# A recommender's attention over 200 history rows on Trainium2: another share of rows by address, categories by products, longer loop bodies and a new end

## The chip, the cores and the metric

The kernel runs on one core of a Trainium2 chip. The metric is device microseconds (us) of one execution, lower is better. The kernel before has a median of 31,307.11 us over 12 runs (31,251.07 to 31,361.09).

Engines have these short names: PE (matrix products; PEld is its loading of weights), DVE (VectorE), ACT (ScalarE), POOL (GpSimd), SP (SyncE, which here only issues DMAs). SBUF is the memory on the chip that the engines work from, and PSUM the memory that PE writes to. A DMA is issued by an engine and then runs by itself.

## The reference

The model has a user, an item, a category and 200 earlier items for each of B = 16,384 examples. The tables have rows of D = 64 fp32 numbers (256 bytes): 100,000 items, 100,000 users, 1,000 categories. All is fp32.

```python
def dice(x, alpha, axis):
    mean = jnp.mean(x, axis=axis, keepdims=True)
    var = jnp.var(x, axis=axis, keepdims=True)
    p = jax.nn.sigmoid((x - mean) * jax.lax.rsqrt(var + EPS))
    return x * (p + alpha * (1.0 - p))
u = u_emb[user]                # (B, 64)
it = i_emb[item]               # (B, 64)
c = c_emb[cate]                # (B, 64)
h = i_emb[hist]                # (200, B, 64)
itb = jnp.broadcast_to(it[None], h.shape)
feat = jnp.concatenate([h, itb, h - itb, h * itb], axis=-1)
a = dice(feat @ au_W1 + au_b1, au_alpha, axis=1)     # 256 -> 36
w = a @ au_W2 + au_b2                                # 36 -> 1
cur = jnp.sum(w * h, axis=0)
z = jnp.concatenate([u, it, c, cur], axis=-1)        # (B, 256)
z = dice(z @ W1 + b1, alpha1, axis=0)                # 256 -> 80
z = dice(z @ W2 + b2, alpha2, axis=0)                # 80 -> 40
return z @ W3 + b3                                   # 40 -> 2
```

The mean and variance of the first `dice` go over the whole batch, for each of the 200 history positions by itself. So no gate of a position can be computed before all 16,384 rows of that position have been through the first layer.

## The kernel before, in words

**Tiles and steps.** A position is called l here, 0 to 199. Its 16,384 rows are eight columns c = 0 to 7 of 16 tiles, 128 rows a tile. A step is k = l x 8 + c, 1,600 in all. The rows of a step land in `rows[k % 5]` (`ROWS` = 5), a buffer of 128 partitions x 16 tiles x 64 numbers.

**Two ways to fetch.** (1) *Gathers*: `gather` (L123) is one indirect DMA on POOL's queue, which fetches 128 rows by a list of row numbers in SBUF. (2) *By address*: in `rows_by_address` (L279) an engine loads row addresses into its registers (`values_load_multi_w_load_instructions`, L293, up to `LOAD` = 20 addresses a load) and issues one DMA of 256 bytes for each row (L301). Half of these rows are issued by SP, half by ACT. They land in `side[m % 3]`, 128 rows a tile m, and each adds 16 to the semaphore `landed[m % 3]`. `SIDES` = (1, 3, 4, 5, 6, 7) are the columns whose sixteenth tile goes by address; the tile of column `SOMETIMES` = 5 does so in one of three l only (`has_side`, L315; `EACH` = 3), and otherwise it is gathered by a list of its own, `sidx`. So an l has 6 tiles by address and 122 gathers, or 5 and 123. The 768 or 640 rows by address of an l are split evenly over its eight steps, 96 or 80 a step, half of them SP's and half ACT's: 48 in three loads of 16 addresses, or 40 in two of 20 (a load that would cross from one tile to a tile that doesn't follow it in memory is split).

`await_rows` (L309) waits on ACT until a tile has landed and clears its semaphore; `place` (L346) then copies the tile from `side` to its place in `rows` on ACT (L352).

**One step** (`step`, L383) issues, in this order, for three steps and one far behind: the gathers of k; the bias of step k - 2 (`hidden`, ACT L339, from PSUM `px` to `xs`), and behind the last column of an l its `measure` and `moments`; the sigmoid of step k - 9 (`gate`, ACT L328, `LAG` = 9); the landed tile of k - 1 (`place`); the rows by address of k; for k - 1 the transposes (`turn`, DVE L156) and the first products (L161, PSUM `ph` and `px`); the statistics of k - 2 (`measure`, DVE L344); for k - 1 the product of h and item and its matmul (`product`, L359 to 361); the weights of k - 9 and their sum into `curT` (`weights`, `weigh`, L331, L335, L336). Each engine works through its own part of this list in order. So the ACT queue has, for each step: one `hidden`, one `gate`, possibly one wait with a copy, and its row issues.

`moments` (L363) makes mean and variance of one l from the statistics of its 16 halves on DVE and calls `scale_and_shift` (L167), which takes the square root on ACT (L170) and the reciprocal on DVE.

**The loop.** A hardware loop (`For_i`, L457) runs bodies of `LPB` = 45 l, written out in full: four bodies make 180 l. The last 20 l are written out behind the loop. All engines meet at the end of each body.

**Before the loop** (L425 to 454): row numbers of items, categories and users are loaded (`ids`), attention weights are arranged (`attention_weights`), 128 gathers fetch the item rows, DVE transposes them into `itT`, and the weights of the head are loaded (`head_weights`, DMAs on SP).

**After the loop** (from L486): the last 20 l, then 256 gathers for categories and users (`head_fetch`, L471, one step of 16 tiles for each column and table), the layer 256 -> 80 (`head_layer`, L477), its two `dice` (`head_moments` L503, once for 64 and once for 16 of the 80 units; `dice` L522), the layer 80 -> 40, its `dice`, the last layer, transposes back, and the output in 14 DMAs at the very end (L562, L568).

Of the kernel before, what the change touches and what calls it, by code (L numbers as in the profile page):

```python
# [14 lines left out]
P = 128  # L15
D = 64
# [4 lines left out]
LPB = 45  # L21
# [7 lines left out]
LOAD = 20  # L29
# [5 lines left out]
def din_kernel(  # L35
# [76 lines left out]
    ids = [make(f"ids{i}", P, NT, dt=I32) for i in range(3)]  # L112
# [17 lines left out]
    def load_ids(t, v):  # L130
        nc.sync.dma_start(t[:, :NC], columns(v))
        for s in range(NS):
            nc.sync.dma_start(t[:, NC + s : NC + s + 1], col(v[(NC + s) * P : (NC + s + 1) * P]))

# [9 lines left out]
    def load_addresses(i, l):  # L144
        nc.sync.dma_start(addr[i], r_hist[ds(l, 1), NC * P :])
# [21 lines left out]
    def scale_and_shift(mean, var, rstd, shift):  # L167
        n = mean.shape[0]
        std = small.tile([P, 1], F32, tag="std", name="std")
        nc.scalar.activation(std[:n], var, AF.Sqrt, bias=eps[:n])  # L170
        nc.vector.reciprocal(rstd, std[:n])
        nc.vector.scalar_tensor_tensor(shift, mean, -1.0, rstd, ALU.mult, ALU.mult)

    eps = make("eps", P, 1)
# [14 lines left out]
    def attention_weights():  # L189
        nc.vector.memset(eps, EPS)  # L190
# [45 lines left out]
    def head_weights():  # L236
# [3 lines left out]
        for e in range(2):  # L240
            for g in range(2):
                r, d = quarter(e, g), ts(e, S)
                nc.sync.dma_start(w1a[r, :, ts(g, ZA)], w1[d, :, :ZA])
                nc.sync.dma_start(w1b[r, :, ts(g, ZB)], w1[d, :, ZA:])
        for g in range(2):
            nc.sync.dma_start(w2a[ts(g, ZA), g * ZA : g * ZA + Z2], W2[:ZA])
# [20 lines left out]
    flat = i_emb.rearrange("v d -> (v d)").bitcast(U8)  # L267

# [4 lines left out]
    def tiles_by_address(l):  # L273

        round_, i = divmod(l, EACH)
        first = round_ * (EACH * (NS - 1) + 1) + i * (NS - 1) + (i > 0)
        return first, [j for j, c in enumerate(SIDES) if has_side(l * ND + c)]

    def rows_by_address(k):  # L279
        l, s = divmod(k, ND)  # L280
        first, tiles = tiles_by_address(l)
        n = len(tiles) * P // ND // 2
        loads = -(-n // LOAD)
        for i, (engine, issue) in enumerate(
            ((mybir.EngineType.SP, nc.sync), (mybir.EngineType.Activation, nc.scalar))
        ):
            r0, end = (2 * s + i) * n, (2 * s + i + 1) * n
            while r0 < end:
                many = min(end - r0, -(-n // loads))
                at0 = tiles[r0 // P] * P + r0 % P  # L290
                while tiles[(r0 + many - 1) // P] * P + (r0 + many - 1) % P != at0 + many - 1:
                    many -= 1
                _, at = nc.values_load_multi_w_load_instructions(  # L293
                    addr[l % 3][:, at0 : at0 + many],
                    engines=(engine,), min_val=0, max_val=ROW * (V - 1),
                    skip_runtime_bounds_check_because="the DMA checks the address against the table",
                )
                for r, a in enumerate(at, r0):
# [9 lines left out]

    def await_rows(m):  # L309
        if m in keys:  # L310
            fence = nc.scalar.wait_ge(landed[m % 3], 16 * P)
            tc.declare_fence(fence.ins, group=keys.pop(m))
            nc.scalar.sem_clear(landed[m % 3])

    def has_side(k):  # L315
        l, c = divmod(k, ND)
        return c in SIDES and (c != SOMETIMES or l % EACH == 0)
# [28 lines left out]
    def place(k):  # L346
        if has_side(k):
            l, c = divmod(k, ND)
            first, tiles = tiles_by_address(l)
            m = first + tiles.index(SIDES.index(c))  # L350
            await_rows(m)
            nc.scalar.copy(rows[k % ROWS][:, TD - 1], side[m % 3])  # L352
# [30 lines left out]
    def step(k, last=None):  # L383
# [12 lines left out]
        if has(k - LAG):  # L396
            gate(k - LAG)
        if has(k - 1):
            place(k - 1)
        if has(k):  # L400
            rows_by_address(k)
        if has(k - 1):
# [5 lines left out]
        if has(k - LAG):  # L408
# [3 lines left out]
    def steps(l0, n, end):  # L412
        for k in range(n * ND):
            l, c = divmod(k, ND)
            if c == 0 and l + 1 < end:
                load_hist_ids((l + 1) % IDX, l0 + l + 1)
                if (l + 1) % EACH:
                    load_side_ids((l + 1) % IDX, l0 + l + 1)
            if c == 2 and l + 1 < end:
                load_addresses((l + 1) % 3, l0 + l + 1)  # L420
            if c == 4 and l + 1 < end:
                scale_addresses((l + 1) % 3)
            step(k)

    with tc.manual_schedule():  # L425
        load_ids(ids[0], r_item)
        load_hist_ids(0, 0)
        load_addresses(0, 0)
        load_ids(ids[1], r_cate)
        load_ids(ids[2], r_user)  # L430
        nc.gpsimd.iota(lanes, pattern=[[1, P]], base=P, channel_multiplier=-1)
        attention_weights()
        for t in (*hT, *xs, *side, hm):
            nc.vector.memset(t, 0.0)  # L434
        for t in curT:
# [7 lines left out]
        scale_addresses(0)  # L443
        layer(px, [(blk_m, hm)])

        for c in range(ND + 1):
            if c < ND:
                for n in range(TD):
                    j = column(c, n)
                    gather(rows[c % ROWS], ids[0][:, j : j + 1], n, i_emb)  # L450
            if c:
                transpose(itT[c - 1], rows[(c - 1) % ROWS])
        nc.vector.memset(rows[-1 % ROWS], 0.0)
# [13 lines left out]
    def measure_head(i, j, t):  # L467
        for h in range(2):
            nc.vector.bn_stats(zst[i][:, 2 * j + h, :], t[:, ts(h, CH)])

    def head_fetch(k, j):  # L471
        c, u = divmod(j, 2)
        for n in range(TD):
            i = column(c, n)
            gather(rows[k % ROWS], ids[1 + u][:, i : i + 1], n, (c_emb, u_emb)[u])

    def head_layer(j):  # L477
        c, u = divmod(j, 2)
        if u == 0:
# [121 lines left out]
```

## Time and profile before

| what | number |
|---|---|
| median of 12 runs | 31,307.11 us |
| the profiled execution's own time | 31,272.79 us |
| its span, first to last instruction | 31,271.0 us |
| granted TensorE clock | 0.805 of full speed |
| gathers of history rows by `idx` / by `sidx` | 24,400 / 133 |
| gathers by `ids` (items, categories, users) | 3 x 128 |
| rows issued by address, SP / ACT | 68,288 / 68,288 |
| DMA engines, mean busy share | about 0.1; 28 GB/s from HBM |
| start of the last gather | 31,167.99 us |

How to read the profile: each engine has a row of busy time, its share of the span, and its number of instructions; a group of instructions is named by its line, engine, operation and output <- inputs. Idle time is put down to what ended it, "<-". "issue" is idle time in which the engine waited for nothing that the profile shows, its own preparation of the next instruction among it. `ACTq` and `SPq` are the DMA queues that ACT and SP feed; a row of such a queue in the timeline gives the start, the length and the number of issues of one uninterrupted stretch. The times of PE's and POOL's instructions are partly modelled; starts are more exact than lengths.

The four joins between bodies show on POOL as longer distances between two gathers: 27.52, 5.29, 5.71 and 4.10 us.

### The profile page before, as it was taken

What the parts mean: (1) busy time and instruction counts of PE and PEld (TensorE: products, weight loads), DVE (VectorE), ACT (ScalarE), POOL (GpSimd) and SP (SyncE); (2) the same over time, 40 slices, a digit from 0 to 9 for tenths busy, and PEclk for the clock granted to TensorE, in tenths of its full rate; (3) what the DMA queues carried; (4) which work ended last, traced back from release to release, by engine and by line L of the source; (5) the groups of instructions that cost most, each with busy time, mean ns of one, the idle gap of its engine ahead of it and who ended that gap; (6) DMA issues with size and microseconds to landing.
All of it is one profiled execution on the core that took longest, in us unless ns stands there. A gap on an engine that the chain in (4) does not pass through costs nothing. (4 is left out here: it accounts for less than half of the span.)

```text
span 31271.0 us, 423966 instructions
## 1 busy us (share of the span) xinstructions
PE 20699.5 (66%) x38856; PEld 8494.9 (27%) x38856; DVE 15126.9 (48%) x18955; ACT 4403.3 (14%) x4941; POOL 23526.3 (75%) x24922
## 2 busy tenths in 40 slices
PE   5666666666666666666666666666666666666666
PEld 2222222222222222222222222222222222222222
DVE  4444444444444444444444444444444444444444
ACT  1111111111111111111111111111111111111111
POOL 7777777777777777777777777777777777777776
PEclk8878877887788788887888878878878888877887
DMA  1111111111111111111111111111111111111111
GB/s 29 29 29 29 29 29 29 29 29 28 29 29 29 29 29 29 29 29 29 29 29 29 29 29 29 29 29 29 29 29 29 29 29 29 29 29 29 29 29 24
DMA packets 1130924, 894.71 MB, mean 29 GB/s; under 512 B 729024, under 2 KB 729024, under 8 KB 1127896
## 3 DMA queue, kind: packets, MB, share of 16 engines
q0 software_dynamic: 797344, 818.07, 11.8%
q1 hardware_dynamic: 193112, 31.56, 0.6%
q10 hardware_dynamic: 137440, 17.76, 0.4%
q14 instruction: 2722, 22.30, 0.2%
q8 instruction: 306, 5.01, 0.1%
HBM read 865.10 MB, written 0.13 MB: 28 GB/s over the span
## 5 line engine op out<-in xcount | busy, mean ns | idle before, releaser
L123 POOL DMA_INDIRECT rows<-in_L_rec_i_emb,idx x24400 | 23037.9, 944 | 7486.6 <-issue 7213.7
L161 PE MATMUL ph<-hT,unit 128*128 128x512 f32 x6404 | 5890.2, 1067 | 10372.5 <-DVE hT L156 10370.6
L335 DVE SCALAR_TENSOR_TENSOR wb<-wb,au_bias,hT 128x1024 f32<-128x1024 f32 x1609 | 2079.7, 1293 | 10852.8 <-PE wb L161 10852.8
L156 DVE STREAM_TRANSPOSE hT<-rows 64x512 f32<-64x512 f32 x6404 | 4515.1, 705 | 2591.5 <-ACT rows L352 1877.1
L339 ACT ACTIVATE xs<-px,au_bias 128x1024 f32<-128x1024 f32 x1602 | 1783.5, 1113 | 25585.4 <-issue 11742.9
L161 PEld LDWEIGHTS ph<-hT,unit 128*128 128x128 f32 x6404 | 1722.5, 302 | 13401.0 <-DVE hT L156 13234.8
L161 PE MATMUL px<-hT,blk_h 128*128 128x512 f32 x6404 | 4111.5, 731 | 0.1
L161 PE MATMUL px<-itT,blk_i 128*128 128x512 f32 x6404 | 3338.4, 603 | 0.0
L161 PE MATMUL wb<-y,blk_p 128*128 128x512 f32 x6436 | 3295.2, 594 | 29.8 <-DVE y L331 29.8
L161 PE MATMUL wb<-xs,blk_x 128*128 128x512 f32 x6436 | 3293.3, 593 | 5.3 <-DVE curT L336 5.3
L161 PE MATMUL px<-hm,blk_m 128*128 128x512 f32 x6408 | 3013.0, 592 | 40.6 <-DVE hm L434 40.6
L360 DVE TENSOR_TENSOR hm<-ph,itT 128x1024 f32<-128x1024 f32 x1601 | 1960.2, 1224 | 1903.3 <-PE ph L161 1903.3
L161 PEld LDWEIGHTS px<-hT,blk_h 128*128 128x128 f32 x6404 | 1644.2, 257 | 2407.3 <-issue 2398.3
L344 DVE BATCH_NORM_STATS2 st<-xs 128x6 f32<-128x512 f32 x3204 | 2060.5, 685 | 290.6 <-ACT xs L339 245.7
L336 DVE TENSOR_TENSOR curT<-wb,curT 128x1024 f32<-128x1024 f32 x1609 | 1969.7, 1224 | 54.8
L331 DVE TENSOR_TENSOR y<-pg,xs 128x1024 f32<-128x1024 f32 x1609 | 1952.8, 1214 | 2.3 <-ACT pg L328 2.2
L161 PEld LDWEIGHTS px<-itT,blk_i 128*128 128x128 f32 x6404 | 1395.8, 218 | 2024.0 <-issue 2024.0
L328 ACT ACTIVATE pg<-xs,sh,rs 128x1024 f32<-128x1024 f32 x1609 | 1934.3, 1202 | 22.4 <-DVE y L331 17.4
L161 PEld LDWEIGHTS wb<-y,blk_p 128*128 128x128 f32 x6436 | 1224.9, 190 | 1575.3 <-issue 1539.7
L161 PEld LDWEIGHTS px<-hm,blk_m 128*128 128x128 f32 x6408 | 1217.9, 190 | 1573.3 <-issue 1532.7
L161 PEld LDWEIGHTS wb<-xs,blk_x 128*128 128x128 f32 x6436 | 1223.7, 190 | 1550.5 <-issue 1541.1
L352 ACT COPY rows<-side 128x64 f32<-128x64 f32 x1068 | 249.2, 233 | 328.9 <-DMA side<-in_L_rec_i_emb 197.2
(155 smaller groups left out, 2190.5 us busy)
## 6 DMA issues: line engine op xcount, KB each, us to landing
side<-in_L_rec_i_emb SPq DMA_DIRECT2D x68288, 0.2 KB
side<-in_L_rec_i_emb ACTq DMA_DIRECT2D x68288, 0.2 KB
rows<-in_L_rec_i_emb,idx POOLq DMA_INDIRECT x24400
idx<-in_r_hist SPq DMA_DIRECT2D x200, 61.0 KB
addrs<-in_r_hist SPq DMA_DIRECT2D x200, 3.0 KB
sidx<-in_r_hist SPq DMA_DIRECT2D x133, 0.5 KB
rows<-in_L_rec_i_emb,sidx POOLq DMA_INDIRECT x133
rows<-in_L_rec_i_emb,ids POOLq DMA_INDIRECT x128
```

Source lines behind the costliest of these rows:

```text
L123: nc.gpsimd.indirect_dma_start(out=dst[:, n, :], out_offset=None, in_=table, in_offset=bass.IndirectOffsetOnAxis(ap=ids, axis=0),)
L156: nc.vector.transpose(by_tile(dst[ts(e, D)], i), of[ts(i, D), :, ts(e, S)])
L161: nc.tensor.matmul(dst[:, ts(i, CH)], lhsT, rhs[:, ts(i, CH)], start=(first and j == 0), stop=(last and j == len(pairs) - 1), skip_group_c ...
L328: nc.scalar.activation(pg, xs[k % XR], AF.Sigmoid, bias=shifts[i], scale=rstds[i])
L331: nc.vector.tensor_mul(y, pg, xs[k % XR])
L335: nc.vector.scalar_tensor_tensor(wb, wb, au_bias2, hT[k % LAG], ALU.add, ALU.mult)
L336: nc.vector.tensor_add(curT[k % ND], wb, curT[k % ND])
L339: nc.scalar.activation(xs[k % XR], px, AF.Identity, bias=au_bias)
L344: nc.vector.bn_stats(stats[l % 3][:, 2 * c + i, :], xs[k % XR][:, ts(i, CH)])
L352: nc.scalar.copy(rows[k % ROWS][:, TD - 1], side[m % 3])
L360: nc.vector.tensor_mul(hm, ph, itT[k % ND])
```

## The change

1. **The loop**: `LPB` goes from 45 to 90, so that two bodies make the 180 l.
2. **The sixth tile**: with the new `MOST` = 2, column 5 goes by address in two of three l.
3. **Loads**: `LOAD` goes from 20 to 24, and the list of loads is made by `shares`.
4. **Order in a step**: SP asks for all of its rows (`ask_hist(k, 0, ...)`), ACT for the first of its two parts, then follows `gate`, then ACT's second part, and then the landed tile is placed.
5. **The landed tile** is awaited and copied on DVE, in place of ACT.
6. **The root**: `scale_and_shift` makes 1 / sqrt on DVE, from a shifted integer as the first guess and three Newton steps, in place of the square root on ACT and a reciprocal.
7. **Items and users**: of their tables, too, the tiles of `SIDES` go by address (`ask_all`, `place_tile`; the last of the users' is gathered through `sidx`).
8. **Categories**: there are no gathers for them. Before the loop, `pick_categories` compares the category numbers of 1,024 examples, spread over 125 partitions, with 8 x 125 category numbers (DVE), and multiplies the ones and zeros with the table (PE), 16 times 8 comparisons and 16 products of 125 x 64 x 512. The results go over ACT to `stages` and by DMA to `catT` in DRAM, from where the end reads them back, a column at a time.
9. **The end**: one pass of 8 columns over the users, in which a second step of `weigh` is done for each column from the third on, `head_layer` in two calls, evacuations in halves, the two normalizations of 64 and 16 units in one chain (`start_moments`, `end_moments`), some of `dice` in two parts and some of its work on ACT (`scalar`), and the first half of the output sent before the last column.

```diff
-LPB = 45
+LPB = 90
...
-LOAD = 20
+MOST = 2
+LOAD = 24
+SPLIT = 0.5
...
     def scale_and_shift(mean, var, rstd, shift):
...
-        nc.scalar.activation(std[:n], var, AF.Sqrt, bias=eps[:n])
-        nc.vector.reciprocal(rstd, std[:n])
...
+        nc.vector.tensor_scalar_add(v, var, EPS)
+        nc.vector.tensor_single_scalar(h.bitcast(I32), v.bitcast(I32), 1, ALU.logical_shift_right)
+        nc.vector.tensor_scalar(
+            rstd.bitcast(I32), h.bitcast(I32), -1.0, float(0x5F375A00), ALU.mult, ALU.add
+        )
+        for _ in range(3):
+            if n == 1:
+                nc.vector.scalar_tensor_tensor(h, rstd, v, rstd, ALU.mult, ALU.mult)
...
+            nc.vector.tensor_scalar(h, h, -0.5, 1.5, ALU.mult, ALU.add)
+            nc.vector.tensor_mul(rstd, rstd, h)
         nc.vector.scalar_tensor_tensor(shift, mean, -1.0, rstd, ALU.mult, ALU.mult)
...
+    def shares(n, s, split):
+
+        many = round(n * split)
+        runs = []
+        for r0, end in ((s * n, s * n + many), (s * n + many, (s + 1) * n)):
+            loads = -(-(end - r0) // LOAD)
+            at = [r0 + (end - r0) * i // loads for i in range(loads + 1)]
+            runs.append(list(zip(at, at[1:])))
+        return runs
...
+    def ask_hist(k, queue, some):
+        l, s = divmod(k, ND)
+        first, tiles = tiles_by_address(l)
+        runs = shares(len(tiles) * P // ND, s, SPLIT)[queue]
+        ask(queue, runs[some], first, tiles, addr[l % 3], i_emb)
...
     def await_rows(m):
         if m in keys:
-            fence = nc.scalar.wait_ge(landed[m % 3], 16 * P)
+            fence = nc.vector.wait_ge(landed[m % 3], 16 * P)
             tc.declare_fence(fence.ins, group=keys.pop(m))
-            nc.scalar.sem_clear(landed[m % 3])
+            nc.vector.sem_clear(landed[m % 3])
...
-        return c in SIDES and (c != SOMETIMES or l % EACH == 0)
+        return c in SIDES and (c != SOMETIMES or l % EACH < MOST)
...
-            nc.scalar.copy(rows[k % ROWS][:, TD - 1], side[m % 3])
+            place_tile(k, first + tiles.index(SIDES.index(c)))
+
+    def place_tile(k, m):
+        await_rows(m)
+        nc.vector.tensor_copy(rows[k % ROWS][:, TD - 1], side[m % 3])
...
-        if has(k - LAG):
+        if has(k):
+            ask_hist(k, 0, slice(None))
+            ask_hist(k, 1, slice(0, 1))
+        if k - LAG not in weighed:
             gate(k - LAG)
+        if has(k):
+            ask_hist(k, 1, slice(1, None))
         if has(k - 1):
             place(k - 1)
-        if has(k):
-            rows_by_address(k)
-        if has(k - 1):
             turn(k - 1)
...
+    def pick_categories(q):
+        for b in range(NB):
+            ones = xs[(q * NB + b) % XR][:PB]
+            nc.vector.tensor_scalar(
+                ones, spread[q % SPREAD], values[:PB, b : b + 1], None, ALU.is_equal
+            )
+            for g in range(2):
+                nc.tensor.matmul(
+                    bank[q % 8][ts(g, D)], table[:, b], ones[:, ts(g, CH)],
+                    start=b == 0, stop=b == NB - 1, skip_group_check=True,
+                )
+        nc.scalar.copy(
+            stages[q % 4].rearrange("p (n t) -> p n t", t=S),
+            bank[q % 8].rearrange("p (t n) -> p n t", n=TD),
+        )
...
+        for c in range(ND + 1):
+            if c < ND:
+                fetch_all(c, c, ids[0], i_emb)
+                ask_all(c, 0.56, -NS, NS, addr[2], i_emb)
+                for q in (2 * c, 2 * c + 1):
+                    pick_categories(q)
+                    if q + SPREAD - 1 < HALVES:
+                        spread_categories(q + SPREAD - 1)
+                    if q:
+                        store_categories(q - 1)
+            if c == 0:
+                attention_weights()
+                scale_addresses(0)
+            if c:
+                if c - 1 in SIDES:
+                    place_tile(c - 1, SIDES.index(c - 1) - NS)
+                transpose(itT[c - 1], rows[(c - 1) % ROWS])
...
-        for j in range(2 * ND + 2):
-            if j < 2 * ND:
-                head_fetch(K + j, j)
-            step(K + j, last=K - 1)
...
+        for j in range(ND + 2):
+            if j < ND:
+                fetch_all(K + j, j, ids[1], u_emb)
...
+                nc.sync.dma_start(category[j % 2], catT[j])
+            step(K + j, K - 1, weighed)
...
+            if j < ND:
+                ask_all(j, SPLIT, first, NS - 1, U, u_emb)
...
-        na, nb = head_moments(0, same_a), head_moments(1, same_b)
+        start_moments("z", 0, 2, 0, same_a)
+        start_moments("z", 1, 2, 1, same_b)
+        na, nb = end_moments("z", (same_a, same_b))
...
+            if c == ND - 2:
+                finish(0)
+                send(0, (nc.sync, nc.sync))
+        finish(1)
+        send(1, (nc.sync, nc.scalar))
```

## The prediction

> **What bounds the kernel now.** I read the page first, then the waits of POOL, then POOL and ACT in order of time.
>
> ```profile
> span 31271.0 us, 423966 instructions
> PE 20699.5 (66%) x38856; PEld 8494.9 (27%) x38856; DVE 15126.9 (48%) x18955; ACT 4403.3 (14%) x4941; POOL 23526.3 (75%) x24922
> L123 POOL DMA_INDIRECT rows<-in_L_rec_i_emb,idx x24400 | 23037.9, 944 | 7486.6 <-issue 7213.7
> ```
>
> POOL looks 75% busy, but what ends its idle time is "issue", its own preparation of the next gather. The waits of POOL say the same: nothing that another engine does holds a gather for longer than 0.3 us.
>
> ```profile
> POOL rows L123 <- issue: 7363.4, 24006, 26.6
> POOL rows L123 <- DMA rows<-in_L_rec_i_emb,idx: 197.2, 646, 0.3
> ```
>
> The longest wait, 26.6 us, is a loop end. In order of time on POOL:
>
> ```profile
> 7055.52 0.94 POOL L123 DMA_INDIRECT rows<-in_L_rec_i_emb,idx  x1 [0.30 <-issue]
> 7056.77 0.94 POOL L123 DMA_INDIRECT rows<-in_L_rec_i_emb,idx  x1 [0.31 <-issue]
> 7084.29 0.94 POOL L123 DMA_INDIRECT rows<-in_L_rec_i_emb,idx  x1 [26.57 <-issue]
> ...
> 13981.41 0.95 POOL L123 DMA_INDIRECT rows<-in_L_rec_i_emb,idx  x1 [0.30 <-issue]
> 13986.70 0.94 POOL L123 DMA_INDIRECT rows<-in_L_rec_i_emb,idx  x1 [4.34 <-issue]
> ```
>
> From 7084.29 to 13981.41 lie the 5,520 gathers of one body of 45 l (15 with 122, 30 with 123): 6897.12 / 5,519 = 1.2497 us each. Gathers times this period is the time.
>
> The second actor is hidden by the page: the ACT queue, which issues half of the rows fetched by address (here `ACTq L301`).
>
> ```profile
> 4289.53 6.45 ACTq L301 DMA_DIRECT2D side<-in_L_rec_i_emb  x20
> ...
> 4318.04 18.40 ACTq L301 DMA_DIRECT2D side<-in_L_rec_i_emb  x48
> 4336.57 1.11 ACT L339 ACTIVATE xs<-px,au_bias 128x1024 f32<-128x1024 f32 x1 [19.63 <-issue]
> ...
> 4341.36 0.29 ACT L170 ACTIVATE std<-var,eps 128x1 f32<-128x1 f32 x1 [2.38 <-DVE var L380]
> ...
> 4343.41 18.65 ACTq L301 DMA_DIRECT2D side<-in_L_rec_i_emb  x48
> 4362.16 1.11 ACT L339 ACTIVATE xs<-px,au_bias 128x1024 f32<-128x1024 f32 x1 [17.98 <-issue]
> ...
> 4364.56 17.93 ACTq L301 DMA_DIRECT2D side<-in_L_rec_i_emb  x46
> 4382.61 1.11 ACT L339 ACTIVATE xs<-px,au_bias 128x1024 f32<-128x1024 f32 x1 [18.07 <-issue]
> ```
>
> Twenty issues without an address load take 6.45 us, 0.3225 each. 46 issues with two loads of 16 addresses take 17.93, so a load costs (17.93 - 46 x 0.3225) / 2 = 1.55. An ordinary step of an l with six such tiles is 48 x 0.3225 + 3 x 1.55 + 0.35 = 20.5 (4362.16 to 4382.61 is 20.45); POOL needs 122 / 8 x 1.2497 = 19.06 for it. From one six-tile l to the next, three l on (4313.68 to 4774.37 on the same line), ACT takes 460.7 us a round, POOL 368 x 1.2497 = 459.9. The two are level: ACT is the shadow bound, and five row buffers let POOL run ahead of it.
>
> **The change, part by part.** *Gathers.* Before: 24,400 + 133 + 3 x 128 = 24,917 (page, part 6). After: in 134 of 200 l six tiles go by address, so 134 x 122 + 66 x 123 = 24,466; items 122, users 123, categories none: 24,711. That is 206 fewer, x 1.2497 = **-257.4 us**, on the path as long as POOL paces.
>
> *The ACT and SP queues* get 17 x 64 = 1,088 issues a round for 1,024. ACT loses: the wait for the moments (step 4336.57 to 4362.16 is 25.6 against 20.5; over three l 5.1 + 5.5 + 5.2 = 15.9, as the square root and its tables go to DVE and the gate now follows half of the issues) and the wait for landed rows (2.4 + 3.1 + 3.1 = 8.6, which goes to DVE). Loads fall from 58 to 49 but grow to 24 addresses: 20 addresses cost (14.80 - 39 x 0.3225, the stretch at 4298.75) = 2.2 at most and 1.6 in the stretch at 7063.55 (14.20 for 39); I take 1.8, and 2.05 for 24. A six-tile step is then 48 x 0.3225 + 2 x 2.05 + 0.25 = 19.83, a five-tile step 40 x 0.3225 + 2 x 1.8 + 0.25 = 16.75; 16 x 19.83 + 8 x 16.75 + 2.1 (one split load, and 1.4 that the same sum leaves open for the round before) = 453.4. POOL needs 367 x 1.2497 = 458.6. So POOL still paces, by 5 us a round, 1%: **0**, and the cover is thin. SP, with the same issues but without activations, has more room.
>
> *DVE* gets the landing wait, 1,147 copies and, once per l, 13 small operations in place of two, 13 x 0.19 (starts of dependent ones, 31184.92 to 31185.11) = 2.5 us. Behind the wait stand the transposes, then PE, then `hidden` on ACT. The DVE-PE chain of a step is 17.09 (consecutive L335 at 30832.44 and 30849.53); with 0.3 for the copy and 5 us of moments per l it is 8 x 17.4 + 5 = 144 per l, against 152.5 on POOL: **0**.
>
> *Copies beside gathers.* L148 is the nearest DVE operation that disturbs POOL: over its 200 runs the gather under way took 1.273 us to the next, +0.024, worst +0.236. A copy of 128x64 is short (0.23 on ACT, L352, against 0.55): 1,147 x 0.024 x 0.42 = 12. Ends: 0, and 1,147 x 0.236 = 271. Taken **+12**. The Trainium skill speaks against this part: SBUF — State Buffer, section "Who interferes with whom", says that an fp32 copy on VectorE between SBUF tiles can hold the port that GpSimd needs to write descriptors, and that the later of the two waits for the whole instruction. By that rule alone the copies would cost up to 1,147 x 0.23 = 264; the row of L148 shows a tenth of such a wait, and I go by the row.
>
> *Loop ends.* Four joins cost 26.3 + 4.0 + 4.5 + 2.9 (27.52, 5.29, 5.71 and 4.10 between gathers, less 1.25). The first is long because the queues start late and are still behind; this holds after the change too, so two joins stay at 26.3 + 2.9: **-8.5** (ends -33 if the queues catch up within 90 l, +20 if they fall further back).
>
> *Prologue.* The category rows come as 16 x 8 x 2 = 256 products of 512 columns. No row shows this shape; a 512-column product takes two passes, 0.43 apart when PE runs on:
>
> ```profile
> 10002.54 0.19 PEld L161 LDWEIGHTS px<-hm,blk_m 128*128 128x128 f32 x1 [0.24 <-issue]
> 10002.97 0.19 PEld L161 LDWEIGHTS px<-hm,blk_m 128*128 128x128 f32 x1 [0.24 <-issue]
> ```
>
> 256 x 0.86 = 220 us, while 122 gathers last 152. DVE's comparisons are 128 x 0.81 (L525, 128x1024) = 104. DVE does the item transposes between the comparisons, and each must free a row buffer. Products start at about 14 us, stand still from 41 to 48 (DVE waits for `au_w`, behind 54 row issues on SP), and the sixth transposes come at about 48 + 11 x 13.75 + 3 = 202, when POOL wanted that buffer at 155: 47 us, and 9 more for the next: **+56**. Lower end: if products overlap and DVE paces, the buffers come at 147, 182 and 202 (the last two held by SP's rows), which costs 10. I take the row. TensorEngine Tiling (Array Packing), section "Tiling Modes", says that different column tiles work in parallel; these products are 64 columns wide in alternating halves, so by it PE would need 110 us and the sum would be 46 lower. No run here shows it.
>
> *End.* After the last gather (31167.99) follow 103 us. The two normalizations become one chain (31186.57 to 31189.45: -2.9), four L525 go to ACT (4 x 0.81 = 3.2), the first half of the output leaves earlier (about 1.6); the longer root gives back 0.7: **-7** (ends -15, +5).
>
> Sum: 31271 - 257.4 - 8.5 + 56 - 7 + 12 = 31,066 for a profiled execution. This one took 31,272.79, 34 below the median of 31,307.11; 31,066 + 34 = **31,100** for the median.
>
> **Rivals.** *The prologue is hidden* (products in parallel, or POOL's five buffers cover more): 31,100 - 46 = 31,054. For it: DVE's 104 us; against it: every product in the trace keeps its 0.43 a pass.
>
> *ACT becomes the bound, and the kernel slower.* It decides from 5 us a round, which is 5.2 / 1,088 = 0.005 us an issue: at 0.327 ACT is level with POOL, at about 0.330 the gain is gone (67 rounds x 3.1 = 207), and at 0.335, near what the 39 issues from 4383.97 show (16.00 less two loads of 1.55, over 39, is 0.331), a round is 467: 31,100 + 67 x 8.4 = 31,660. Against it: the clean stretches give 0.3225, and the 24 us of waits taken from ACT are measured. A mild form (1 to 3 us a round) ends between 31,170 and 31,300.
>
> *The queues never catch up*: SP and ACT enter the loop some 45 us later than now, and with level rates the join after 90 l costs this too, with no other loss: 31,145.
>
> *Copies hold the gathers* at the upper end: 31,100 + 259 = 31,359, no change. And the change could fail to do what it says: not for the gathers, whose number is fixed in the program.
>
> **How the numbers follow.** Forecast 0.42, prologue hidden 0.25, queues never catch up 0.08, ACT mild 0.12, ACT slower 0.10, copies 0.03. About 0.2% (63 us) can be told from no change. Faster than 31,244: 0.42 + 0.25 + 0.08 + half of 0.12 = 0.81; within: 0.06 + 0.03 = 0.09; slower than 31,370: 0.10. The range goes from 30,995 (hidden prologue, short join and no offset of the median) to 31,300 (the end of the mild ACT case). Predicted 31,100.
>
> **What would show it.** 24,711 gathers at 1.25 us, two joins; gaps of 47 and 9 us on POOL between 150 and 240 us; no `L170` on ACT; ordinary six-tile ACT steps of 19.8. Wrong if gathers in mid-loop wait for DVE's transposes, if ACT's steps exceed 20.1, or if a gather beside a copy takes much over 1.26.

## The result, and the profile after

The changed kernel takes **31,956.81 us** (median of 8 runs, 31,942.03 to 31,966.64), the kernel before 31,278.04 us in the runs beside it: a ratio of **1.0215**, 95% interval 1.0206 to 1.0224. It is slower by 2.15%, where the prediction had 31,100 and gave slower a chance of 0.10.

The page of the changed kernel, its first lines, the row of the gathers, and the row of the copies that went to DVE:

```profile
span 31956.9 us, 445222 instructions
PE 21207.2 (66%) x39376; PEld 8559.2 (27%) x39376; DVE 15842.6 (50%) x22426; ACT 3819.1 (12%) x3317; POOL 23404.5 (73%) x24716
...
L125 POOL DMA_INDIRECT rows<-in_L_rec_i_emb,idx x24400 | 23087.3, 946 | 8244.1 <-issue 7217.2
...
L386 DVE COPY rows<-side 128x64 f32<-128x64 f32 x1146 | 242.3, 211 | 1050.8 <-DMA side<-in_L_rec_i_emb 1042.0
```

The gathers cost the same each (946 ns for 944), but POOL's idle time has grown from 7,487 to 8,244 us. The waits of POOL say by what (engine, line, what it waited for: us in total, times, longest):

```profile
POOL rows L125 <- issue: 7308.7, 23655, 59.9
POOL rows L125 <- DVE hT L153: 558.7, 146, 7.4
POOL rows L125 <- DMA rows<-in_L_rec_i_emb,idx: 261.2, 698, 1.6
POOL rows L125 <- DVE itT L153: 77.9, 3, 64.0
```

Before, no gather waited more than 0.3 us for another engine. Now POOL stands 559 us until DVE's transposes (L153) have emptied a row buffer: POOL no longer sets the pace.

Where the 685.9 us between the two profiled spans come from, by the starts of gathers (the time of each part less its gathers at 1.2497 us, after less before):

| part | us |
|---|---|
| 206 gathers fewer, at 1.2497 | -257.4 |
| bodies of the loop, beyond their gathers (+389.0 and +229.4; before: -5.7) | +624.1 |
| joins: two of 62.7 and 60.8 against 27.5, 5.3, 5.7 and 4.1, less one period each | +83.4 |
| before the loop (239.1 us up to its first gather, for 122 x 1.2497 = 152.5) and the start | +87.7 |
| the last 20 l, and the gathers behind them | +70.1 |
| after the last gather (177.2 us against 99.3) | +78.0 |

The last gather before the change starts at 31,171.73 us; 31,167.99, given for it above, is the fourth from last.

The loop is the largest of them. A round of three l takes some 460 us before and 471.0 us in the first body after, 467.6 in the second; its gathers need 458.6. Windows over one round of the second body, cut at the `hidden` with which ACT starts the first step of an l (columns: the window, its length, the busy time of PE, PEld, DVE, ACT and POOL with the number of instructions, the granted clock, the DMA share, GB/s):

```profile
20079.20:20241.00 161.80, 104.87 (x194) 41.65 (x192) 80.73 (x112) 18.57 (x16) 122.44 (x130) 0.84 0.13 29
20241.00:20403.20 162.20, 106.64 (x192) 42.65 (x192) 77.92 (x110) 18.58 (x17) 122.45 (x131) 0.81 0.16 29
20403.20:20546.70 143.50, 100.25 (x191) 41.67 (x192) 74.47 (x107) 18.57 (x16) 101.99 (x108) 0.81 0.14 27
```

One round differs from the next by a few us. Averaged over 15 rounds of the second body and cut in the same way, the six-tile l take 160.1 and 160.2 us and the five-tile l 147.3, all three other than what their gathers need (152.5, 152.5, 153.7). PE and DVE work about as long in each. ACT's queue sets the six-tile l: it has 158.4 and 157.3 us of issues and loads in them. In the five-tile l it has only 134.6, and POOL makes only 108 gathers in the window, so something else holds it. In order of time, ACT and its queue at the start of the five-tile l (start, length, what; in brackets the idle time of ACT's arithmetic before it and what ended it):

```profile
20395.42 7.67 ACTq L322 DMA_DIRECT2D side<-in_L_rec_i_emb  x24
20403.19 1.11 ACT L371 ACTIVATE xs<-px,au_bias 128x1024 f32<-128x1024 f32 x1 [8.43 <-issue]
20404.77 7.04 ACTq L322 DMA_DIRECT2D side<-in_L_rec_i_emb  x20
20411.85 1.21 ACT L360 ACTIVATE pg<-xs,sh,rs 128x1024 f32<-128x1024 f32 x1 [7.55 <-DVE hT L153]
20413.49 6.63 ACTq L322 DMA_DIRECT2D side<-in_L_rec_i_emb  x20
20421.29 1.11 ACT L371 ACTIVATE xs<-px,au_bias 128x1024 f32<-128x1024 f32 x1 [8.23 <-PE wb L158]
20422.85 6.55 ACTq L322 DMA_DIRECT2D side<-in_L_rec_i_emb  x20
20430.91 1.21 ACT L360 ACTIVATE pg<-xs,sh,rs 128x1024 f32<-128x1024 f32 x1 [8.50 <-DVE sh L183]
20432.47 6.87 ACTq L322 DMA_DIRECT2D side<-in_L_rec_i_emb  x20
20444.50 1.11 ACT L371 ACTIVATE xs<-px,au_bias 128x1024 f32<-128x1024 f32 x1 [12.38 <-PE wb L158]
```

An ordinary step of this l is 16.9 to 17.4 us. Here the steps from `hidden` (L371) to `hidden` are 18.1 and 23.2: the issues end at 20439.34, and `hidden` starts 5.2 us later. What it waits for is PE's product `wb`: of eight buffers `xs`, steps k - 2 and k - 10 share one, so `hidden` of k - 2 can't write before the product of k - 10, in the step before, has read. And DVE in the same time:

```profile
20400.28 1.23 DVE L368 TENSOR_TENSOR curT<-wb,curT 128x1024 f32<-128x1024 f32 x1
20408.14 0.19 DVE L386 COPY rows<-side 128x64 f32<-128x64 f32 x1 [6.63 <-DMA side<-in_L_rec_i_emb]
20408.56 2.88 DVE L153 STREAM_TRANSPOSE hT<-rows 64x512 f32<-64x512 f32 x4 [0.23 <-DMA rows<-in_L_rec_i_emb,idx]
...
20424.62 1.27 DVE L376 BATCH_NORM_STATS2 st<-xs 128x6 f32<-128x512 f32 x2
20431.09 2.88 DVE L153 STREAM_TRANSPOSE hT<-rows 64x512 f32<-64x512 f32 x4 [0.21 <-issue]
20436.38 1.23 DVE L399 TENSOR_TENSOR hm<-ph,itT 128x1024 f32<-128x1024 f32 x1 [2.41 <-PE ph L158]
20437.53 1.22 DVE L363 TENSOR_TENSOR y<-pg,xs 128x1024 f32<-128x1024 f32 x1
20445.36 1.29 DVE L367 SCALAR_TENSOR_TENSOR wb<-wb,au_bias,hT 128x1024 f32<-128x1024 f32 x1 [6.62 <-PE wb L158]
```

Two delays stand here, in adjacent steps, once an l. DVE waits 6.63 us for the tile of column 7, whose last row ACT issued at 20402.87, right before `hidden`; and a step later statistics and moments (20424.62 to 20431.09) stand ahead of the transposes. Both push the transposes, the products, `y` and `wb` back, and ACT, which can't run a step ahead of them, stands.

Summed over rounds of the second body, ACT's queue has 1,088 issues with 368.5 us, 49 loads with 82.0 and 17.1 us of waits. Of these 12.9 lie in the five-tile l, 1.6 and 2.7 in the others. In the first body it is 376.6, 82.1 and 12.0: there the issues are dearer, and issues and loads together need 458.7 us, as much as POOL's gathers, before any wait.

The 15 rounds also tell the two delays apart. In the round shown the tile landed early. In most it is like this, one round earlier, in order of time:

```profile
19930.52 1.11 ACT L371 ACTIVATE xs<-px,au_bias 128x1024 f32<-128x1024 f32 x1 [8.47 <-issue]
...
19939.93 0.20 DVE L386 COPY rows<-side 128x64 f32<-128x64 f32 x1 [11.15 <-DMA side<-in_L_rec_i_emb]
...
19940.78 6.43 ACTq L322 DMA_DIRECT2D side<-in_L_rec_i_emb  x20
...
19953.38 1.11 ACT L371 ACTIVATE xs<-px,au_bias 128x1024 f32<-128x1024 f32 x1 [13.03 <-PE wb L158]
```

The copy starts 9.4 us after `hidden`. ACT's issues end at 19947.21, and the next `hidden` starts 6.2 us later (5.4 of them are the wait itself). In 12 of the 15 rounds the copy starts 7.3 to 9.4 us after `hidden`, and ACT stands 4.4 to 5.8 us in this step. In the other three it starts after 3.7 to 5.2, and ACT stands 0.8 to 1.8. The wait one step later, behind the moments, is 5.1 to 5.8 us in all 15. So of the five-tile l's waits 4.6 us go with the landing (on average) and 5.5 with the moments; the other six steps have 2.6. In the six-tile l 1.0 and 2.3 lie behind the moments and next to nothing behind the landing.

### The profile page after: what moved, and what is told of

It is laid out like the page before. It is cut to its first block, busy times and chain, and to the rows that moved or that the text cites. A ratio compares the mean times of both kernels' runs of the same rounds, so it can differ in the third digit from the quotient of the medians.

```text
span 31956.9 us, 445222 instructions
## 1 busy us (share of the span) xinstructions
PE 21207.2 (66%) x39376; PEld 8559.2 (27%) x39376; DVE 15842.6 (50%) x22426; ACT 3819.1 (12%) x3317; POOL 23404.5 (73%) x24716
## 4 chain that ended last, share of the span: by engine, by line
POOL 21%; issue 10%; ACTq 8%; PE 6%; DMA 5%; DVE 3%; ACT 2%; DVEq 0%; POOLq 0%
POOL rows L125 21%; ACTq L322 7%; DMA rows<-in_L_rec_i_emb,idx 5%; PE px L158 3%; PE ph L158 2%; PE wb L158 2%; DVE hT L153 1%; ACT pg L360 1%; ACT xs L371 1%; ACTq L314 1%; DVE wb L367 0%; DMA side<-in_L_rec_i_emb 0%; DVE st L376 0%; DVE curT L368 0%; DVE y L363 0%
## 5 line engine op out<-in xcount | busy, mean ns | idle before, releaser
L153 DVE STREAM_TRANSPOSE hT<-rows 64x512 f32<-64x512 f32 x6404 | 4517.5, 705 | 213.8 <-DMA rows<-in_L_rec_i_emb,idx 47.5
L158 PE MATMUL wb<-y,blk_p 128*128 128x512 f32 x6440 | 3457.6, 619 | 1224.7 <-DVE y L363 1222.3
L158 PE MATMUL px<-hT,blk_h 128*128 128x512 f32 x6404 | 4176.6, 742 | 0.0
L371 ACT ACTIVATE xs<-px,au_bias 128x1024 f32<-128x1024 f32 x1602 | 1785.3, 1114 | 14276.1 <-PE wb L158 6272.3
L158 PE MATMUL wb<-xs,blk_x 128*128 128x512 f32 x6440 | 3374.4, 606 | 5.3 <-DVE curT L368 5.3
L386 DVE COPY rows<-side 128x64 f32<-128x64 f32 x1146 | 242.3, 211 | 1050.8 <-DMA side<-in_L_rec_i_emb 1042.0
```

The source lines that it names most:

```text
L153: nc.vector.transpose(by_tile(dst[ts(e, D)], i), of[ts(i, D), :, ts(e, S)])
L158: nc.tensor.matmul(dst[:, ts(i, CH)], lhsT, rhs[:, ts(i, CH)], start=(first and j == 0), stop=(last and j == len(pairs) - 1), skip_group_c ...
L371: nc.scalar.activation(xs[k % XR], px, AF.Identity, bias=au_bias)
```

## The experiments

The comparisons of E1 to E4 ran on one chip, on which the kernel before had a median of 31,322.75 us. The changed kernel itself has no run on record there; where its rounds are set beside those of E1, E3 and E4, the kernels before differ by 0.14% (31,278.04 and 31,322.75). E3 and E4 are single executions. Rounds are those of the second body, where nothing else is said.

**E1: `weigh` off the chain of each step.** Ten buffers `hT` (one of them a buffer that the loop doesn't use otherwise), and `weigh` of a step is issued behind the transposes of the next.

```diff
             turn(k - 1)
+        if pending:
+            weigh(pending.pop())
...
             weights(k - LAG)
-            weigh(k - LAG)
+            if last is None:
+                pending.append(k - LAG)
+            else:
+                weigh(k - LAG)
```

> The changed kernel with one edit: the last part of a step on DVE (weigh, which waits for PE's last product of the step) is issued behind the transposes of the next step, and hT has ten buffers for nine. Theory (coupled chain): in the l with five tiles by address ACT waits for the chain transposes - products - gate - weights - weigh - transposes, some 147.7 us an l, and in the l with six tiles it is ACT's issues, 159.9 an l; one can't make up for the other, so a round of three l costs 2 x 159.9 + 147.7 = 467.6. With weigh off the chain a step of it falls from 17.1 to some 14 us, ACT no longer waits, its own work of 450.5 a round is below the 458.6 of the gathers: rounds of 458 to 460, joins under 30 us each, total 31,100 to 31,260. Rival (dearer issues: ACT's row issues at 0.339 us in place of 0.3225 set the round): rounds stay at 464 or more, total over 31,700. Rival (copies on DVE hold the gathers): rounds between 463 and 468 with POOL's own period longer than 1.255.

Measured: 31,819.82 us, ratio 1.0156 (1.0139 to 1.0173); rounds of 464.9. A window over a five-tile l:

```profile
20334.90:20479.20 144.30, 98.45 (x192) 40.34 (x192) 76.92 (x109) 18.61 (x17) 106.87 (x115) 0.85 0.21 28
```

On average over 15 rounds a five-tile l takes 145.4 us, for 147.3 in the change. Its ordinary steps fell from 17.0 to 16.6 us, so the chain did hold them, but by 0.4 only. ACT's waits are still 15.3 us a round, and still at the two steps shown above (4.7 and 4.4 in the five-tile l). The theory that the chain of every step makes the 17 us fell: the waits fell by 1.8 us and the round by 2.7. The numbers are those that the rival of dearer issues forecast (rounds of 464 or more, over 31,700 us). In the second body issues and loads add up to 449 us a round, so there they alone don't make 464.9. In the first body they take 459 of 469.4, so there this rival is not refuted. What is left in the second body are the once-an-l delays.

**E2: the sixth tile in one of three l again.**

```diff
-MOST = 2
+MOST = 1
```

> The changed kernel with the sixth tile by address in one of three l again, all else as changed. Theory (coupled chain): a round costs max over its l, 159.9 + 2 x 147.7 = 455.3, under the 368 x 1.2497 = 459.9 of the gathers, so POOL paces: rounds of 460, total 24,778 x 1.2497 = 30,965 + 87 (first gathers) + 30 (joins) + 34 + 150 (end) = about 31,270. Rival (copies on DVE hold the gathers, or the new prologue and end cost it all): rounds stay over 464 and the total over 31,600.

Measured: **31,267.28 us**, ratio **0.9972** (0.9958 to 0.9987): 0.3% faster than the kernel before, and as the theory had it (about 31,270). Its waits of POOL:

```profile
POOL rows L125 <- issue: 7297.2, 23886, 0.3
POOL rows L125 <- DMA rows<-in_L_rec_i_emb,idx: 174.1, 570, 0.3
POOL rows L125 <- DVE itT L153: 77.4, 3, 62.3
```

The wait for `hT` is gone; rounds are 460.7 (368 gathers at this chip's 1.252), the joins 5.7 and 3.9 us. ACT has 33.7 us of waits a round and they cost nothing, since POOL needs longer. What is left of the slowdown is in front and behind: 77 us of POOL's waits for `itT`, and 129 us after the last gather, for 99 before.

**E3: gate in front of all row issues.**

```diff
+        if k - LAG not in weighed:
+            gate(k - LAG)
         if has(k):
             ask_hist(k, 0, slice(None))
-            ask_hist(k, 1, slice(0, 1))
-        if k - LAG not in weighed:
-            gate(k - LAG)
-        if has(k):
-            ask_hist(k, 1, slice(1, None))
+            ask_hist(k, 1, slice(None))
```

> The changed kernel with gate in front of all row issues of the step, as before the change. Theory (coupled chain): in ordinary steps gate comes 9.7 us earlier, which the five-tile l can't use (y waits for product on DVE), while in the step of the moments ACT waits some 5.9 us for the shift again: rounds of 470 to 482, total 32,050 to 32,600. Rival (the late gate itself is what holds the five-tile l): rounds of 462 or less, total under 31,600.

Measured: 32,709.51 us, rounds of 478.5 (483.5 in the first body), so the total is above the theory's range. The rival is out. ACT's waits are 30.0 us a round, and nearly all of them are one wait an l, at the gate behind the moments: 7.6 and 8.3 us in the six-tile l, 9.7 in the five-tile l, where 1.8 more lie a step earlier; every other step has 0.1. Here the moments are priced by themselves: some 26 us a round where ACT meets them with no issue in between. With the late gate the round is some 11 us shorter.

**E4: the kernel before with the sixth tile in two of three l**, nothing else changed (`MOST = 2` in `has_side`, `tiles_by_address` and `steps`).

> The kernel before with one edit, the sixth tile by address in two of three l. Theory (coupled chain): a six-tile l of the kernel before takes ACT 172 us, a five-tile l 144.5, so a round is 2 x 172 + 144.5 = 488, total about 33,000: the sixth tile is the part that slows, and the other parts win some of it back. Rival (gathers pace, and something else in the change slows): rounds of 458.6, total about 31,150.

Measured: 33,018.16 us, rounds of 486.5, all four joins of 63 to 65 us. So the sixth tile alone costs the kernel before 5%, as the sum over its own l says (171.1 + 171.2 + 144.3 measured), and the other parts of the change take 19 us a round off that.

**The later runs, and other chips.** E5 to E8 and all that follow fell on five other chips, an hour and more later, and there the kernel before itself takes 51,008 to 51,426 us. Whether that lies in the chips or in something else that had changed by then isn't shown: no chip is on record with both. Nor has the changed kernel itself a run there. Nothing of the loop's balance can be carried over, so each is told in a line. E5, E7, E8, E10, E12, E14 and E15 are single executions.

E5, and again E10, E12 and E15: no moments (mean, variance and root of the loop are left out).

```diff
                 measure(k - 2)
-                moments((k - 2) // ND)
```

> The changed kernel without moments (no mean, no variance, no root in the loop; the gate works with scale and shift zero; the statistics of each half are still taken). Theory, as the first runs leave it (moments stall): once an l DVE does 7.4 us of statistics and small operations between hidden and the transposes; ACT, which can run less than a step ahead, waits for it at the next two hidden, 10 us and more in a five-tile l and 1 to 2 in a six-tile l. Without moments a round is ACT's own 450 or the gathers' 458.6: rounds of 458 to 461, total 31,080 to 31,250. Rival (the chain of every step, or dearer issues, holds the five-tile l): rounds of 464 or more, total over 31,650.

> The kernel of e5 again, without moments. Theory (moments stall): rounds of 458 to 461 and a total 0.2 to 0.6% under the kernel before on the same chip. Rival (the chain of every step, or dearer issues, holds the five-tile l): rounds of 464 or more, slower by 1% or more.

> The changed kernel without moments, a third time, in the hope of a chip with the usual pace of row issues. Theory (moments stall): rounds of 458 to 461 and a total 0.2 to 0.6% under the kernel before on the same chip. Rival (the chain of every step, or dearer issues, holds the five-tile l): rounds of 464 or more, slower by 1% or more.

> The changed kernel without moments. Theory (two delays at the start of an l): the waits of ACT fall to 6 a round or less, rounds of 458 to 461, a total 0.2 to 0.6% under the kernel before on the same chip. Rival (the chain of every step, or dearer issues): rounds of 464 or more, slower by 1% or more.

Measured: 52,626.25 us beside 51,369.25 (1.0245), then 1.0250, 1.0260 and 1.0244; rounds of 773 to 778 us. By the letter the rival came true four times, slower by over 1%; but rounds this long fit neither side, whose 458 to 464 are for the usual pace of issues.

E6, and again E9, E11, E13, E16 and E17: both delays off the path, nothing left out. To E1 come nine buffers `xs`, and in the step of the moments the order transposes, `weigh`, `product`, statistics and moments, and the gate behind all row issues.

```diff
-XR = 8
+XR = 9
...
         if has(k - 1):
             product(k - 1)
+        if ends:
+            measure(k - 2)
+            moments((k - 2) // ND)
+            if gates:
+                gate(k - LAG)
```

> The changed kernel with the moments moved off the path, nothing left out: in the step of the moments the transposes, weigh and product come first and the gate stands behind all of ACT's issues; weigh is issued behind the next transposes (ten buffers hT); nine buffers xs, so that hidden doesn't wait for the product of the step before. Theory (moments stall): no wait on ACT over 1 us, rounds of 458.6 to 460.5, joins under 15 us, total 31,100 to 31,250, faster than the kernel before by 0.2 to 0.6%. Rival (the moments hold the queue wherever they stand, since gate must wait for them): rounds of 463 or more, total over 31,600.

> The kernel of e6 again: the first time the chip itself issued rows so slowly (before: 51,369 us) that nothing of the loop could be read. Theory (moments stall): no wait on ACT over 1 us, rounds of 458.6 to 460.5, joins under 15 us, faster than the kernel before on the same chip by 0.2 to 0.6%. Rival (the moments hold the queue wherever they stand, since gate must wait for them): rounds of 463 or more, slower by 1% or more. If row issues of this chip are slow again, nothing follows.

> The kernel of e6 a third time, in the hope of a chip that issues rows at its usual pace (before near 31,300 us). Theory (moments stall): no wait on ACT over 1 us, rounds of 458.6 to 460.5, joins under 15 us, faster than the kernel before on the same chip by 0.2 to 0.6%. Rival (the moments hold the queue wherever they stand): rounds of 463 or more, slower by 1% or more.

> The kernel of e6 a fourth time. Theory (moments stall): no wait on ACT over 1 us, rounds of 458.6 to 460.5, joins under 15 us, faster than the kernel before on the same chip by 0.2 to 0.6%. Rival (the moments hold the queue wherever they stand): rounds of 463 or more, slower by 1% or more.

> The kernel of e6 on whatever chip is to be had. Theory (two delays at the start of an l, both off the path here): no wait on ACT over 1 us, rounds of 458.6 to 460.5, joins under 15 us, faster than the kernel before on the same chip by 0.2 to 0.6%. Rival (the moments hold the queue wherever they stand): rounds of 463 or more, slower by 1% or more.

> The kernel of e6 once more. Theory (two delays on DVE at the start of an l, the landing of the last tile and the moments, both off the path here): on a chip on which the kernel before takes some 31,300 us no wait on ACT over 1 us, rounds of 458.6 to 460.5, joins under 15 us, 0.2 to 0.6% faster than the kernel before. Rival (the moments hold the queue wherever they stand): rounds of 463 or more, slower by 1% or more. Where the kernel before takes over 51,000 us: 1.06 of it again.

Measured: 54,520.63 us beside 51,369.25, ratio 1.0611 (1.0594 to 1.0629), and 1.0610 to 1.0620 in the five repeats; rounds of 806 us. ACT's waits are some 15 us a round, for 60 in E5 on the same chip, but the issues of a round took 715 us for 641 in E5 and 368.5 in the change above. Slower by over 1%, as the rival had it, but again not for its reason. Whether this kernel is faster where issues have their usual pace stays open.

E7: no category products (zeros in their place, so the category's part of the head is missing).

> The changed kernel without the category products, their comparisons and the 16 transfers of 500 KB that spread the numbers (zeros are stored in their place and read back at the end). Theory: these hold the prologue, in which an address load takes 4.8 us for 1.7 and a column 35 us for the gathers' 19; without them the first gather of the loop comes at 155 to 175 us in place of 243, and as the queues pace the loop and start as much earlier, the total falls by 60 to 110, to 31,850 to 31,900. Rival (the prologue hides behind the queues' lag): total within 25 of 31,957.

Measured: 52,402.45 us beside 51,369.25. The loop's first gather came at 284 us and not at 155 to 175. In E5, with the products, it came at 335 on the same chip: 51 us of the prologue are theirs there. An address load of ACT there took 4.8 us all the same, so that figure isn't theirs.

E8: the root on ACT and the reciprocal on DVE.

> The changed kernel with the square root on ACT and the reciprocal on DVE again. Theory (moments stall): DVE's list is 2 us shorter, but ACT stands some 8 us an l before its row issues until the variance is there, as before the change: rounds of 474 to 486, total 32,300 to 33,000. Rival (the small operations on DVE are what costs): rounds of 464 or less, total under 31,750.

Measured: 52,528.03 us beside 51,369.25; rounds of 776 us, neither forecast can be judged.

E14: the tile of column 7 placed behind the transposes of its column (so that one tile in 16 of that column works with rows of another step).

```diff
-            place(k - 1)
+            late = (k - 1) % ND == SIDES[-1]
+            if not late:
+                place(k - 1)
             turn(k - 1)
+            if late:
+                place(k - 1)
```

> The changed kernel with the landed tile of column 7 put into its buffer behind the transposes of that column instead of ahead of them (so that tile's rows come too late, and column 7 works with other rows in one tile). Theory (two delays at the start of an l): DVE waits 5 to 6.6 us for the tile whose last rows ACT has only just issued, and one step later works 7.2 us at the moments; ACT stands for what exceeds its own step. Without the first the waits of ACT fall from 17.1 to 10 to 12 a round: rounds of 460 to 463 where row issues have their usual pace. Rival (the moments alone): rounds stay at 467 to 468.

Measured: 53,190.32 us beside 51,401.87; rounds of 786 us, so this too tells nothing of the landing.

What these chips do differently shows in E12 itself. First POOL, then ACT's queue, both in order of time:

```profile
20032.92 0.94 POOL L125 DMA_INDIRECT rows<-in_L_rec_i_emb,idx  x1 [0.30 <-issue]
20042.25 0.94 POOL L125 DMA_INDIRECT rows<-in_L_rec_i_emb,idx  x1 [8.39 <-DVE hT L153]
```

```profile
20033.06 9.17 ACTq L322 DMA_DIRECT2D side<-in_L_rec_i_emb  x24
...
20044.17 20.63 ACTq L322 DMA_DIRECT2D side<-in_L_rec_i_emb  x24
```

While POOL stands (20033.9 to 20042.3), 24 issues take 9.17 us; while it gathers, 20.63. Over E15, an ACT issue less its register move takes 0.29 us on average beside an idle POOL and 0.52 beside a gathering one, and the long ones are 0.7, 1.4 or 2.1 us. In the profile of the change they are 0.27 and 0.28.

## Why the prediction was wrong, point by point

**The step that failed** is the sum for the ACT queue: "16 x 19.83 + 8 x 16.75 + 2.1 ... = 453.4 ... So POOL still paces, by 5 us a round". Its total for issues and loads came close, 450.5 us in the second body, but by two errors that cancel. The 0.3225 us an issue was read from one stretch of 20; over the loop before the change the mean was 0.334, and after it is 0.339, which makes 17 us a round more. The loads were put at some 100 us and measure 82. What was set to nothing and isn't is the waits: "ACT loses: the wait for the moments ... and the wait for landed rows (2.4 + 3.1 + 3.1 = 8.6, which goes to DVE)". ACT did lose both waits by name and met them again a step later, mostly in `hidden`, as 17.1 us a round. 450.5 + 17.1 = 467.6, 9 above POOL's 458.6. In the first body the issues cost 0.346 each, and issues and loads alone reach POOL's 458.6; there 12 us of waits come on top. The prediction's own first sign of being wrong, gathers in mid-loop that wait for DVE's transposes, is what the profile shows (558.7 us).

**Why that was missed:** "8 x 17.4 + 5 = 144 per l, against 152.5 on POOL: 0" compared DVE's chain with POOL's mean. It had to be compared with the engine that runs beside it in that l: ACT's own five-tile l is 8 x 16.75 = 134, and ACT can't use up the difference before or after, since `hidden` needs the `px` and the `xs` buffer of the step before. The price of a round is the sum of what each l takes, 160.1 + 160.2 + 147.3, not the longest of three sums. The words "which goes to DVE" had the answer in them: that the wait goes to the engine that feeds ACT was not followed further. The profile of the change shows both delays, and by their place in 15 rounds some 5 us of the 17 go with the landing and some 9 with the moments. No run at the usual pace of issues took either away by itself: those meant for it fell on the slow chips. E1 shows that the chain of ordinary steps makes 2 to 3 us, E3 that ACT loses 7.6 to 9.7 us an l when it meets the moments undisguised, and E2 and E4 that the sixth tile is what turns the order round.

**What followed from it:** the rival "ACT becomes the bound" was what happened. That its round of 467 ("31,100 + 67 x 8.4 = 31,660") is also the measured one is luck. Issues did cost more than its 0.335 us, but the loads cost 20 us a round less than it reckoned with, and waits made up the rest. The remaining 300 us were not in it. The bodies and the last 20 l lost 694 us and not 563, mostly because the first body took 471.0 a round. With DVE some 60 us behind POOL at every body's end, the joins cost 62.7 and 60.8 us ("two joins stay at 26.3 + 2.9"), and the end waits for the same lag (+78 where -7 was forecast). In E2, where POOL paces, the joins are 5.7 and 3.9.

**Gathers:** 24,711, as counted, -257.4. **Copies beside gathers:** in E2 the gather under way at a copy takes 1.268 us to the next on average, the others 1.251: 18 us over all 1,079 copies, for the +12 forecast. It isn't spread evenly: 76 of 1,064 such gathers take 1.35 to 1.63 us, and none of 23,405 others over 1.28 (joins, and one wait of 3.4 us, left out). So a copy can hold a gather, but only one in fourteen did. By the port rule of the Trainium skill alone (SBUF — State Buffer, "Who interferes with whom"), the prediction's estimate was up to 264 us. The 18 measured are far from that; most copies here delayed no gather. **Prologue:** +87 for +56. The products were not the bound: two halves of 64 columns run together,

```profile
56.76 1.88 PE L504 MATMUL ph<-xs,curT 125*64 125x512 f32 x8
```

eight passes in 1.88 us, 0.43 for each pair, and not 0.43 each as the row of full-width products. That different column tiles work in parallel is what the Trainium skill says (TensorEngine Tiling (Array Packing), "Tiling Modes"). A column takes 35 to 36 us there, where the gathers need 19. ACT's 42 row issues and two address loads take 25 of these, and, beside them, SP's 54 issues and three loads 25 to 27. PE's products stand until ACT, behind its issues, has copied a result out:

```profile
80.36 8.54 PE L504 MATMUL ph<-xs,curT 125*64 125x512 f32 x32 [20.00 <-ACT ucT L508]
```

So the trace points to ACT's queue; no run tests it. **The end** by itself did get shorter: in E2, 74 us from the first aggregation of the head's statistics to the end, 87 before. But in the single pass over the users each column from the third on has two sums of `weigh`, and these columns follow each other at 20.1 to 22.2 us, up to the last but one, where the gathers need 19. The chain of the last column starts 55 us after the last gather and not 12.

## What to carry to other kernels

When engines hand buffers to each other within a step, add up the longest engine of each stretch, not each engine's total: two stretches that are each bound by another engine cost both excesses. A wait that is moved from one engine to another is paid by whoever waits for that engine next; follow it until it meets slack. And before shifting more work to a second actor, look whether that one has any slack left: before, the two were level to 0.2%, and one more tile per three l was enough to turn the order round. Last, take the cost of an issue from the mean over the loop and not from its cleanest stretch; a sum can come out right although its terms are wrong.

## What the runs showed of the hardware that was not expected

The same body of code issued rows at 0.260 us (median from an issue to the next move) in its first pass and at 0.251 in its second, and a round was 471.0 and 467.6 us. In 15 rounds of the second body, the tile of column 7 of the l before the five-tile l was complete 4 to 9.5 us after ACT had issued its last row. An address load costs ACT 1.37 us for 16 addresses, 1.50 for 20, 1.79 for 24 in the loop (medians), but 4.8 us for 21 before the loop, where SP's loads of 18 take 1.7. And in the later runs, on other chips, row issues of ACT and SP take longer beside POOL's gathers (E15: 0.29 us beside an idle POOL; 0.52 for ACT and 0.55 for SP beside a gathering one). The mix of both ways to fetch was level on one chip; the same kernel before took 1.6 times as long there, and of the kernels run there E6, with the fewest waits on ACT, was the slowest.
